# Four graph layers on one core: layer 1's output is computed by its width, and nodes 2p and 2p+1 share a partition

## The chip, the cores and the metric

The kernel runs on one core of a Trainium2 chip. The metric is device time in microseconds of one whole execution; the median of several executions is given. A profile is one execution with its instruction trace.

## The reference

64 graphs of 256 nodes with 512 features pass through four layers. Each layer normalises `x` by node, applies relu to give `h`, and adds the layer's result to `x`:

```python
h = jnp.maximum(_layernorm(x, axis=-1), 0.0)
x = x + layer(h, adj, ...)
```

Layers 0 and 3 compute one number per node from the adjacency matrix and two projections of `h`, take a softmax of it over the nodes, and scale a third projection, `v`, by it. Layer 2 has eight heads of 64 features: `tanh(A * (Xp C) Xp^T) Xp`, then relu.

Layer 1, which the change is mostly about, is attention with eight heads of 64 features:

```python
dense = leaky_relu(e_self[..., :, None] + e_neigh[..., None, :], 0.2) + NEG_BIG * (1.0 - A)
att = softmax(dense, axis=-1)
out = relu(einsum('bhij,bhju->bhiu', att, feats) + b)
```

`e_self` and `e_neigh` are one number per node and head. All data is float32.

## The kernel before

One graph is one pass of `graph(b)`, a set of named steps. Each step issues its instructions when it is called; the table `TIMES` gives each step a due time, and `Plan.run` calls the steps of all graphs sorted by `b * PERIOD + due`. On each engine and on SP's queue of transfers the instructions then run in just that order, so the table is the schedule: about five graphs are in flight, and only the order of the due times counts, not their values. Buffers (PSUM banks, tiles of x, and so on) come from fixed pools through `take` and go back with `done`, in that same order.

A graph's nodes lie on the partitions: chunk `c` of 128 nodes, node `128c + p` on partition `p`. Every layer begins with `normed`: `st`, `rs`, `sh` on VectorE (`bn_stats`, L314), `pw` on GpSimd (L325), `hn` on ScalarE (L337). TensorE needs `h` with the features on the partitions. That turn is made in three steps: `sq` turns 32 by 32 squares on VectorE (L270), `sw` writes them to device memory (L357, tile `sq_d`), and `ht` gathers them back in four transfers (L275). `rows` (L264) is the helper for all products of `ht` with a weight.

Layer 1's steps, in order:
- `fa`, `fb`, `fae`, `fbe`: the features and, in 16 more columns, `e_self` and `e_neigh`. `feats` carries a column of ones behind each head.
- `sendp`, `senda`, `er`, `enes`: TensorE turns the 16 columns into rows (L482), ScalarE copies them (L487), and SP writes them out and broadcasts them to all partitions.
- `max`, `mxv`, `mxp`, `mxa`, `mr`, `mb`: the row maximum on VectorE (L510), turned by TensorE (L531), copied (L536), written and broadcast.
- `ea` (ScalarE, L555), `eg` (GpSimd, L562), `eb` (VectorE, L568), `ex` (ScalarE, L574): the weights of two heads, with the source node on the partitions.
- `po` (TensorE, L586): the exponentials are the stationary operand, and 65 columns of `feats` (64 and the ones) move. The sum of a row thus falls out as the 65th column, with the output node on the partitions.
- `pn` (VectorE, L599 and L603) takes the reciprocal of the sums, and relu and product; `pa` (GpSimd, L611) adds to `x`.

Layer 2's `py` (L690) already works the other way round: features are stationary, 64 wide, two heads go to the two halves of the output's partitions, and 256 nodes move. Its output has the features on the partitions and is turned back by `sqy` (L724), `swy` and `yr` (L736), and added by `yg` and `yv` (L743). `xc` (L655) multiplies by layer 2's matrix C, with one 64 by 64 block for each head; `ps` (L676) are layer 2's scores.

Layers 0 and 3 end with `softp` (TensorE, L375), `softv`, `softa`, `softw` and `add` (L400), with the products `pv`; `z` and `zv` (L783) are layer 3's score. `load` and `store` are SP's transfers of `x` and the adjacency matrix. Before the first graph, ScalarE's queue loads the weights (L172 to L238), and TensorE multiplies the two halves of layer 3's weight.

Of the kernel before, what the change touches and what calls it, by code (L numbers as in the profile page):

```python
# [23 lines left out]
UE = U + 1  # L24
# [12 lines left out]
PERIOD = 60.200  # L37
TIMES = {
    "load": 0.000, "at": 1.247, "st0": 5.280, "rs0": 5.300, "negt": 7.670, "pw0": 13.367, "sh0": 13.387,
    "hn0": 13.407, "sq0": 13.427, "sw0": 16.594, "ht0": 18.551, "qk1": 23.168, "qk0": 24.945, "qe0": 24.965,  # L40
    "qe1": 24.985, "pv01": 25.815, "score0": 27.291, "s0v": 27.311, "softp0": 29.436, "pv00": 31.771,
    "softv0": 32.366, "softa0": 33.344, "softw0": 35.861, "add0": 35.881, "st1": 39.861, "rs1": 39.881,
    "pw1": 40.011, "sh1": 40.031, "hn1": 40.638, "sq1": 43.586, "sw1": 46.132, "ht1": 57.350, "fa0": 57.370,
    "fa1": 57.370, "fb0": 57.370, "fae0": 57.934, "fae1": 58.840, "sendp": 58.860, "senda": 58.880,
    "er": 60.959, "neg": 61.845, "fb1": 64.147, "fbe0": 67.381, "enes": 67.749, "fbe1": 71.535,
    "max2": 74.244, "ea1": 75.256, "max0": 75.757, "max3": 76.069, "ea3": 77.200, "ea0": 78.017,
    "max1": 78.219, "mxv": 78.317, "mxp": 79.925, "ea2": 80.651, "eg2": 82.397, "mxa": 85.102, "eg0": 86.489,
    "mr": 87.558, "eg1": 88.075, "mb": 88.185, "eb0": 90.739, "eb2": 93.202, "ex0": 94.320, "eb1": 95.449,
    "eg3": 96.405, "po0": 97.573, "ex1": 97.708, "ex2": 99.827, "po2": 100.283, "eb3": 101.293,
    "ex3": 101.313, "po1": 102.298, "pn0": 106.351, "pa0": 108.061, "po3": 110.560, "pn1": 110.580,  # L50
    "pa1": 114.029, "st2": 114.049, "rs2": 114.069, "pw2": 114.089, "sh2": 117.872, "hn2": 117.892,
    "sq2": 120.365, "sw2": 126.933, "ht2": 134.926, "xp0": 134.946, "xp1": 140.660, "xe0": 141.890,
    "xe1": 147.360, "sqx": 147.380, "swx": 148.833, "xpt": 152.315, "xc": 161.371, "xcv": 174.104,
    "ps0": 174.124, "xca": 174.124, "tv1": 174.144, "ta1": 174.164, "tv0": 174.656, "ta0": 177.182,
    "ps1": 177.255, "tv2": 177.275, "ta2": 178.752, "tv3": 180.071, "am": 180.091, "ta3": 180.091,
    "py0": 181.534, "py1": 184.516, "ye0": 188.391, "ye1": 188.411, "sqy": 190.648, "swy": 192.764,
    "yr": 197.444, "yv": 199.505, "yg": 201.580, "st3": 202.086, "rs3": 203.471, "pw3": 205.848,
    "sh3": 205.868, "hn3": 207.396, "sq3": 207.856, "agg0": 209.112, "sw3": 211.920, "ga0": 215.679,
    "agg1": 217.655, "ht3": 218.179, "ga1": 220.247, "z0": 234.444, "z1": 245.189, "zv0": 245.866,
    "pv30": 248.297, "pv31": 251.239, "zv1": 261.554, "softp3": 263.233, "softv3": 264.096,  # L60
    "softa3": 267.934, "softw3": 282.911, "add3": 285.241, "store": 294.897,
}


class Plan:

# [8 lines left out]
    def run(self, graph, count):  # L75
        graphs = {}
        for _, b, name in sorted((b * PERIOD + at, b, name) for b in range(count) for name, at in TIMES.items()):
            if b not in graphs:
                graphs[b] = graph(b)
            traced = self.tc.nc.cur_bb.bb.instructions  # L80
            n = len(traced)
            graphs[b].steps[name]()
            for i in traced[n:]:
                if i.engine in PINNED:
                    if i.engine in self.last:
                        self.tc.add_manual_dep(i, self.last[i.engine], mybir.DependencyInfo(
                            mybir.DependencyClass.NoSync, mybir.DependencyReason.DATA), reason="plan")
                    self.last[i.engine] = i.name
# [32 lines left out]
def tile_four_gnn_layers(ctx: ExitStack, tc: tile.TileContext, x, adj, nodemask,  # L121
# [4 lines left out]

    nc = tc.nc
# [7 lines left out]
    small = ctx.enter_context(tc.tile_pool(name="small", bufs=6))  # L135
# [4 lines left out]
    plan = Plan(tc)  # L140

# [11 lines left out]
    keep("blocks", 2, [P, NC, N // S, S])  # L153
    keep("feats", 2, [P, NC, H, UE])
# [5 lines left out]
    keep("o", 1, [P, NC, 4 * U])  # L160
    turn = [0]

    def passing(name):
        turn[0] += 1
        return plan.pools["bank"][4 + turn[0] % 4]

    def load_weight(name, src):
        t = consts.tile([P, KC, src.shape[1]], F32, name=name)  # L170
        for r in range(4):
            nc.scalar.dma_start(t[r::4], src.rearrange("(k r d) e -> r d k e", k=KC, r=4)[r])  # L172
        return t
# [5 lines left out]
    for f in plan.pools["feats"]:  # L179
        nc.gpsimd.memset(f[:, :, :, U:], 1.0)  # L180

    wqk0_s = load_weight("wqk0_s", wqk0)
    wv0_s = load_weight("wv0_s", wv0)
    w1a_s = consts.tile([P, KC, FA], F32)
    w1b_s = consts.tile([P, KC, D - HA * U], F32)
    for k in range(KC):
        for r in range(4):
            first = k * P + r * S
            w1_k = w1[:, first:first + S, :].rearrange("h d u -> d h u")
            nc.scalar.dma_start(w1a_s[r::4, k, E:].rearrange("p (h u) -> p h u", h=HA), w1_k[:, :HA])  # L190
            nc.scalar.dma_start(w1b_s[r::4, k].rearrange("p (h u) -> p h u", h=H - HA), w1_k[:, HA:])
    a_bc = once.tile([P, 2, D], F32, bufs=1)
    nc.scalar.dma_start(a_bc[:, 0, :], a_self.rearrange("h u -> (h u)").partition_broadcast(P))
    nc.scalar.dma_start(a_bc[:, 1, :], a_neigh.rearrange("h u -> (h u)").partition_broadcast(P))
    b1_bc = consts.tile([P, D], F32)
    nc.scalar.dma_start(b1_bc, b1.rearrange("h u -> (h u)").partition_broadcast(P))
    mask_rows = once.tile([B, N], F32, bufs=1)
    nc.scalar.dma_start(mask_rows, nodemask)
    w2_s = consts.tile([P, KC, H, U], F32)
    for k in range(KC):  # L200
        for r in range(4):
            first = k * P + r * S
            nc.scalar.dma_start(w2_s[r::4, k], w2[:, first:first + S, :].rearrange("h d u -> d h u"))
    b2_bc = consts.tile([P, D], F32)
    nc.scalar.dma_start(b2_bc, b2.rearrange("h u -> (h u)").partition_broadcast(P))

    c2_s = consts.tile([P, HP, U], F32)
    for s in range(2):
        nc.scalar.dma_start(c2_s[s * U:(s + 1) * U], c2t.rearrange("(a s) k j -> s k a j", s=2)[s])
    wv3_s = load_weight("wv3_s", wv3)  # L210

    for k in range(KC):
        for s in range(2):
            for first, w in ((0, w1a_s[:, k, E:]), (HA, w1b_s[:, k])):
                w = w.rearrange("p (h u) -> p h u", u=U)
                n = w.shape[1]
                prod = once.tile([P, n, U], F32, name="prod", bufs=1)
# [58 lines left out]
    def graph(b):  # L278
# [311 lines left out]
        for p in range(HP):  # L590
            attention(p)
# [237 lines left out]
```

## Time and profile before

| | |
|---|---|
| median of 3 executions | 3979.25 us (3978.55 to 3984.05) |
| profiled execution, its own time | 3981.05 us |
| its span in the trace | 3979.0 us |
| mean granted TensorE clock | 0.989 |
| busy: TensorE, VectorE, ScalarE, GpSimd | 96%, 76%, 43%, 32% |
| DMA packets | 1657995, of them 1494320 under 512 B; 717.69 MB |

The busy shares are of the whole span. A float32 matmul appears as two records in the trace, so counts of matmuls are twice those of the code; the turns by the identity appear once. A group line of the profile names the line, engine, operation and tiles, the shapes, the count, then busy time and mean duration, and last the engine's idle time before the group and what ended it. The timeline of SP lists transfers by the time at which SP issues them, and the second number there is what issuing took, not what the transfer took.

### The profile page before, as it was taken

The page shows a single profiled execution, that of the slowest core. Times are in us where ns is not written, and L with a number is a line of the kernel's source. Part 1 is how long each engine was busy: PE and PEld are TensorE (multiplying, and loading weights), DVE is VectorE, ACT ScalarE, POOL GpSimd, SP SyncE. Part 2 cuts the span into 40 slices and gives each one's busy share as a digit, 9 for nine tenths or more (in the row PEclk, how much of TensorE's full clock was granted, in tenths as well). Part 3 has the DMA queues.
Part 4 walks back from the last instruction along what each step waited for, and adds up shares of the span by engine and source line. Part 5 has one row for each costly group of instructions (what it writes and reads, how often), then busy time and mean ns, then how long its engine had stood idle before and what let it go on. Part 6 is the DMA issues. An engine that isn't in the chain of part 4 may idle for free.

```text
span 3979.0 us, 54683 instructions
## 1 busy us (share of the span) xinstructions
PE 3819.5 (96%) x17986; PEld 2345.2 (59%) x17986; DVE 3023.1 (76%) x7658; ACT 1708.5 (43%) x3333; POOL 1263.1 (32%) x1097
## 2 busy tenths in 40 slices
PE   3689999999999999999999999999999999999997
PEld 1456666656656656656656656656656656665653
DVE  2577878877877878777787787787787887887873
ACT  0344444444444444444444444444444444444442
POOL 0233333332332332332332332332333333333330
PEclk9799999999999999999999999999999999999999
DMA  4577777777877877777777777778777787787763
GB/s 112 136 181 177 195 194 180 192 189 188 185 186 191 187 186 188 185 190 190 178 192 185 181 192 189 176 193 193 171 196 193 175 195 191 180 193 188 184 159 79
DMA packets 1657995, 717.69 MB, mean 180 GB/s; under 512 B 1494320, under 2 KB 1549680, under 8 KB 1633136
## 3 DMA queue, kind: packets, MB, share of 16 engines
q1 hardware_dynamic: 1641472, 706.39, 72.8%
q10 hardware_dynamic: 16240, 7.80, 0.8%
q8 instruction: 144, 2.36, 0.3%
q14 instruction: 139, 1.14, 0.1%
HBM read 477.56 MB, written 236.45 MB: 179 GB/s over the span
## 4 chain that ended last, share of the span: by engine, by line
PE 83%; DVE 7%; DMA 4%; SPq 2%; issue 1%; POOL 1%; ACT 1%; ACTq 1%; POOLq 0%; DVEq 0%
PE bank L264 49%; PE bank L586 11%; PE bank L676 6%; PE bank L690 6%; PE bank L762 5%; PE bank L655 3%; DVE junk L510 3%; DVE sq L270 2%; DMA hn<-sq_d 1%; SPq L275 1%; PE bank L426 1%; DMA ht<-sq_d 1%; PE bank L375 1%; DVE shift L330 1%; POOL xt L743 1%
## 5 line engine op out<-in xcount | busy, mean ns | idle before, releaser
L264 PE MATMUL bank<-wv_s,ht 128*128 128x512 f32 x2048 | 910.8, 592 | 0.0
L264 PEld LDWEIGHTS bank<-wv_s,ht 128*128 128x128 f32 x2048 | 380.9, 191 | 428.6 <-issue 413.1
L562 POOL TENSOR_TENSOR pair<-pair,negt 128x1024 f32<-128x1024 f32 x256 | 598.7, 2361 | 28.7 <-ACT pair L555 28.7
L337 ACT ACTIVATE hn<-xt,shift,rstd 128x512 f32<-128x512 f32 x512 | 390.4, 809 | 458.2 <-DVE shift L330 443.1
L555 ACT ACTIVATE pair<-all,ec 128x256 f32<-128x256 f32 x1024 | 417.1, 496 | 222.1 <-DMA all<-er_d 222.1
L586 PEld LDWEIGHTS bank<-feats,pair 128*128 128x128 f32 x4096 | 473.0, 192 | 58.5 <-issue 53.9
L264 PE MATMUL bank<-w_s,ht 128*128 128x512 f32 x1024 | 466.1, 598 | 33.6 <-DMA ht<-sq_d 28.1
L715 ACT ACTIVATE pair<-pair 128x512 f32<-128x512 f32 x512 | 295.9, 625 | 452.1 <-DVE pair L708 452.1
L586 PE MATMUL bank<-feats,pair 128*128 128x65 f32 x4096 | 479.2, 275 | 2.7 <-ACT pair L574 2.7
L264 PE MATMUL bank<-m_s,ht 128*128 128x512 f32 x1024 | 468.5, 600 | 3.0 <-DMA ht<-sq_d 3.0
L510 DVE CUSTOM_DVE_ANT_0 junk<-all,adj 128x256 f32<-128x256 f32 x1024 | 432.4, 422 | 37.7 <-DMA all<-er_d 4.2
L325 POOL TENSOR_TENSOR rstd<-rstd,power 128x2 f32<-128x2 f32 x256 | 180.5, 705 | 829.1 <-DVE rstd L321 822.6
L708 DVE TENSOR_TENSOR pair<-bank,at 128x512 f32<-128x512 f32 x512 | 328.5, 684 | 127.4 <-PE bank L676 127.4
L743 POOL TENSOR_TENSOR xt<-xt,hn 128x512 f32<-128x512 f32 x64 | 111.7, 1746 | 957.1 <-DMA hn<-sq_d 711.2
L270 DVE STREAM_TRANSPOSE sq<-hn 128x512 f32<-128x512 f32 x512 | 338.1, 690 | 59.4 <-ACT hn L337 59.4
L314 DVE BATCH_NORM_STATS2 stats<-xt 128x6 f32<-128x512 f32 x512 | 327.6, 682 | 28.1 <-POOL xt L743 27.9
L264 PEld LDWEIGHTS bank<-w_s,ht 128*128 128x128 f32 x1024 | 189.2, 192 | 258.6 <-issue 209.8
L568 DVE TENSOR_TENSOR pair<-pair,all 128x1024 f32<-128x1024 f32 x256 | 328.0, 1301 | 0.0
L264 PEld LDWEIGHTS bank<-m_s,ht 128*128 128x128 f32 x1024 | 189.7, 190 | 213.7 <-issue 206.6
L611 POOL TENSOR_TENSOR xt<-xt,o 128x256 f32<-128x256 f32 x256 | 182.7, 725 | 331.2 <-DVE o L603 233.8
L264 PE MATMUL bank<-w1a_s,ht 128*128 128x272 f32 x1024 | 256.1, 404 | 23.6 <-DMA ht<-sq_d 23.6
L754 POOL TENSOR_SCALAR at<-at,mask_c 128x256 f32<-128x256 f32 x128 | 117.5, 927 | 497.7 <-DVE pair L708 497.7
(81 smaller groups left out, 4871.3 us busy)
## 6 DMA issues: line engine op xcount, KB each, us to landing
sq_d<-sq SPq DMA_DIRECT2D x384, 512.0 KB
ht<-sq_d SPq DMA_DIRECT2D x1024, 128.0 KB
all<-er_d SPq DMA_DIRECT2D x128, 1024.0 KB
all<-m_d SPq DMA_DIRECT2D x64, 1024.0 KB
xt<-in_x_dram SPq DMA_DIRECT2D x64, 512.0 KB
xpt<-sq_d SPq DMA_DIRECT2D x256, 128.0 KB
hn<-sq_d SPq DMA_DIRECT2D x256, 128.0 KB
out_dram<-xt SPq DMA_DIRECT2D x64, 512.0 KB
```

Source lines behind the costliest of these rows:

```text
L264: nc.tensor.matmul(p, ht[:, k, c * P:(c + 1) * P], w[:, k], start=(k == 0), stop=(k == KC - 1))
L270: nc.vector.transpose(sq.rearrange("p (r k c i) -> p c k r i", r=4, k=KC, c=NC)[:, c], t[:, c])
L314: nc.vector.bn_stats(stats[:, c, :], g["xt"][:, c, :])
L337: nc.scalar.activation(hn[:, c, :], g["xt"][:, c, :], AF.Relu, bias=st["shift"][:, c:c + 1], scale=st["rstd"][:, c:c + 1])
L510: nc.vector.tensor_tensor_reduce(junk, g["en"][:, h, :], g["adj"][:, c, :], 1.0, -BIG, OP.add, OP.max, st["mx"][:, c, h:h + 1])
L555: nc.scalar.activation(e[:, s, j, :], g["es"][:, h, :], AF.Prelu, bias=st["ec"][:, j, H + h:H + h + 1], alpha=0.2)
L562: nc.gpsimd.tensor_tensor(e, e, g["negt"][:, None].to_broadcast([P, 2, NC, N]), OP.add)
L568: nc.vector.tensor_tensor(e, e, g["m"][:, 2 * p:2 * p + 2, None, :].to_broadcast([P, 2, NC, N]), OP.subtract)
L586: nc.tensor.matmul(po[:, h % 4, :], e[:, s, j, i * P:(i + 1) * P], feats[:, j, h, :], start=(j == 0), stop=(j == NC - 1))
L676: nc.tensor.matmul(ps[s][:, m, :], g["xpt"][half, p, m * P:(m + 1) * P], g["xc"][half, p, :], start=True, stop=True)
L708: nc.vector.tensor_tensor(th[:, s], g[f"ps{p}{s}"].rearrange("p (m n) -> p m n", m=NC), g["at"], OP.mult)
L715: nc.scalar.activation(g[f"th{p}"][:, s], g[f"th{p}"][:, s], AF.Tanh)
```

## The change

- Node `2p + c` lies on partition `p` as chunk `c`. So two neighbouring nodes share a partition, the rows of `x` and of the adjacency matrix are read and written as one run for each partition, and the gathers move runs of 64 elements for 32. A chunk of nodes within a free dimension is now every second element (`chunk`). The 32 by 32 turns write or read in steps of two elements.
- `po` has the features stationary, 64 columns on one half of the output's partitions, and moves the 256 exponentials, like `py`. The column of ones goes. The row sums come from a new matmul, `su`, with a column of ones in a stationary operand of 32 columns; GpSimd first adds the two halves of the source nodes (`eh`). Each pair of a head's position and r has its own 32 output partitions.
- ScalarE takes the output out of PSUM with relu (`oe`), and `back`, now shared with layer 2, turns it to the nodes: `sqo` (VectorE), `swo` and `or` (SP). The sums are copied (`se`), turned by TensorE (`sp`), and inverted by VectorE (`sr`). GpSimd multiplies and adds to `x` (`oa`).
- The score rows and the maxima are turned by VectorE's 32 by 32 transposes (`send`, `mxt`) in place of TensorE and a copy by ScalarE; `er` and `mr` then write in four transfers for one.
- `xc` uses one 128 by 128 block with two heads on its diagonal for two 64 by 64 blocks.
- The weights' steps are issued from SP's queue ahead of the first graph, in a table `WEIGHTS`; before, they were issued from ScalarE's queue.
- Two scratch tiles go (the softmax exponentials and the score products are written over their PSUM source), `small` pools have 5 buffers for 6, and all due times are new, with `PERIOD` 59.0 for 60.2.

```diff
-PERIOD = 60.200
+PERIOD = 59.0
 TIMES = {
...
+    "fa0": 67.715, "fa1": 67.725, "fae0": 67.735, "fae1": 70.445, "send": 70.465, "er": 70.485, "enes": 70.505,
...
+    "ex0": 105.783, "eb2": 106.779, "ex3": 108.073, "po0": 109.204, "eg1": 110.015, "ex2": 111.923, "eb1": 113.549,
+    "po2": 113.901, "eh0": 114.929, "ex1": 117.816, "po1": 117.836, "eh1": 117.837, "oe0": 117.856, "su0": 118.502,
+    "eh3": 118.704, "po3": 119.010, "eh2": 119.242, "su1": 119.262, "oe1": 120.178, "sqo": 120.198, "se": 122.147,
+    "swo": 124.057, "sp": 125.389, "sr": 125.409, "or": 127.489, "oa1": 132.474, "oa0": 135.453, "st2": 135.705,
+    "rs2": 135.725, "pw2": 135.745, "sh2": 135.765, "hn2": 135.785, "sq2": 137.857, "sw2": 137.877, "ht2": 144.252,
...
+    "agg1": 237.211, "ga1": 241.253, "zv0": 241.622, "z1": 250.036, "zv1": 254.364, "softp3": 254.784,
...
+    "store": 284.217,
 }
...
+    def chunk(t, c):
+        return t.rearrange("p (n c) -> p c n", c=NC)[:, c]
...
+    def rows(p, ht, c, w):
+        for k in range(KC):
+            nc.tensor.matmul(p, chunk(ht[:, k], c), w[:, k], start=(k == 0), stop=(k == KC - 1))
+    def squares(sq, t):
+        for c in range(NC):
+            nc.vector.transpose(sq.rearrange("p (r k i c) -> p c k r i", r=4, k=KC, c=NC)[:, c], t[:, c])
+    def gathered(t, sq_d):
+        for i in range(4):
+            nc.sync.dma_start(t.rearrange("p k (b e) -> b p k e", b=4)[i],
+                              sq_d.rearrange("(b d) (r k e) -> b (d r) k e", b=4, r=4, k=KC)[i])
...
+        def back(name, cols):
+            @step(f"sq{name}")
+            def _():
+                nc.vector.transpose(g.take("sq").rearrange("p (b k c i) -> p k b c i", b=4, k=HP, c=NC),
+                                    g[cols].rearrange("p k (b i c) -> p k b c i", b=4, c=NC))
...
+            @step(f"{name}r")
+            def _():
+                y = g.take("hn", NC, name="y" if name == "y" else "yo")
+                y = y.rearrange("p c d -> p (c d)").rearrange("p (a f) -> p a f", a=4)
+                for q in range(4):
+                    nc.sync.dma_start(y[q * S:(q + 1) * S], st["sq_d"].rearrange("(a i) (q f) -> q i a f", a=4, q=4)[q])
...
+        @step("send")
+        def _():
+            st["er"] = er = work.tile([P, N // 4], F32, name="er", bufs=1)
+            nc.vector.transpose(er.rearrange("p (i c) -> p c i", c=NC), st["ec"])
...
-                    po = g[f"po{q}{i}"][:, :4 * UE].rearrange("p (q u) -> p q u", q=4)
                     for s in range(2):
                         h = 2 * p + s
-                        for j in range(NC):
-                            nc.tensor.matmul(po[:, h % 4, :], e[:, s, j, i * P:(i + 1) * P], feats[:, j, h, :],
-                                             start=(j == 0), stop=(j == NC - 1))
+                        nc.tensor.matmul(po[s * U:(s + 1) * U, p % 2, :], feats[:, j, h * U:(h + 1) * U],
+                                         e[:, s, j, :], start=(j == 0), stop=(j == NC - 1))
...
+            @step(f"eh{p}")
+            def _():
+                e = g[f"e{p}"]
+                nc.gpsimd.tensor_tensor(g.take("half", name=f"h{p}"), e[:, :, 0, :], e[:, :, 1, :], OP.add)
...
+            @step(f"su{q}")
+            def _():
+                if not q:
+                    g.take("bank", name="su")
+                for r in range(2):
+                    for s in range(2):
+                        t = 2 * r + s
+                        nc.tensor.matmul(g["su"][t * S:(t + 1) * S, :N], ones[:, q], g[f"h{2 * q + r}"][:, s, :],
+                                         start=(q == 0), stop=(q == 1))
...
+            @step(f"oe{q}")
+            def _():
...
+                nc.scalar.activation(g["oc"][:, 2 * q:2 * q + 2, :], g[f"po{q}"].rearrange("p (r n) -> p r n", r=2),
+                                     AF.Relu)
...
+        def divide(c):
+            @step(f"oa{c}")
+            def _():
+                y = g["yo"].rearrange("p c d -> p (c d)").rearrange("p (a k c i) -> p c k a i", a=4, k=HP, c=NC)[:, c]
+                rs = st["rs"][:, c].rearrange("p q t -> p (q t)").rearrange("p (k s) -> p s k", s=2)
+                for s in range(2):
+                    half = y[:, :, 2 * s:2 * s + 2]
+                    nc.gpsimd.tensor_tensor(half, half, rs[:, s, :, None, None].to_broadcast([P, HP, 2, S]), OP.mult)
+                xt = g["xt"][:, c, :].rearrange("p (k a i) -> p k a i", k=HP, a=4)
+                nc.gpsimd.tensor_tensor(xt, xt, y, OP.add)
```

## The prediction

> **What bounds the kernel now.** I read the page's engine shares first, then the table of windows, the chain of waits through one period, the timeline of SP, and the groups by line.
>
> ```profile
> PE 3819.5 (96%) x17986; PEld 2345.2 (59%) x17986; DVE 3023.1 (76%) x7658; ACT 1708.5 (43%) x3333; POOL 1263.1 (32%) x1097
> ```
>
> ```profile
> 1000.00:2000.00 1000.00, 994.83 (x4743) 613.73 (x4742) 792.17 (x1993) 447.30 (x872) 335.30 (x289) 1.00 0.77 187
> ```
>
> TensorE is busy 99.5% of the middle of the run at clock 1.00. VectorE follows with 79%, DMA with 77%. Busy matmuls are pipelined, so I take what a step adds to the chain:
>
> ```profile
> 2028.45 3.52 PE bank L586 x32
> 2031.97 1.87 PE bank L655 x16
> 2033.84 3.72 PE bank L586 x32
> 2037.56 1.93 PE bank L676 x16
> 2039.49 3.63 PE bank L264 x8
> ...
> 2050.63 0.22 PE bank L482 x2
> 2050.85 3.60 PE bank L690 x32
> ```
>
> A float32 matmul is two records, so `x32` is 16 matmuls. Adding all steps of one graph in this way (pv 4 x 3.44, xp 2 x 3.44, z 2 x 3.44, fa 2 x 1.83, fb 2 x 1.72, qk 2 x 0.89, score0 0.84, agg 2 x 1.75, the softmax turns 0.44, po 7.24, xc 1.87, ps 2 x 1.93, py 3.60, sendp and mxp 0.44) gives **58.2 us of TensorE work per graph**. The x loads of graphs 5 and 63 are issued at 323.6 and 3761.4 in SP's timeline: 58 periods, **59.27 us each**. 541 us lie outside them (fill 324, drain 217). So only 1.1 us per period is not TensorE work. A second limit is close:
>
> ```profile
> 2094.21 0.33 SPq L357 DMA_DIRECT2D sq_d<-sq  x1
> 2096.93 3.80 SPq L275 DMA_DIRECT2D ht<-sq_d  x4
> 2100.83 0.66 SPq L286 DMA_DIRECT2D xt<-in_x_dram  x1
> ```
>
> ```profile
> PE bank L264 <- DMA ht<-sq_d: 56.7, 16, 15.4
> ```
>
> The tile of squares sent out at 2094.21 can be gathered 2.72 us later, the gather takes 3.80 us to issue, and fa0 starts at 2104.99 (TensorE's timeline), just after it lands. The last line (list of waits) is TensorE waiting for such gathers: 57 us in all. The order written by hand leaves little slack behind softp0.
>
> ```profile
> L270 DVE STREAM_TRANSPOSE sq<-hn 128x512 f32<-128x512 f32 x512 | 338.1, 690 | 59.4 <-ACT hn L337 59.4
> L270 DVE STREAM_TRANSPOSE sq<-xp 128x512 f32<-128x512 f32 x128 | 136.6, 1107 | 0.0
> L611 POOL TENSOR_TENSOR xt<-xt,o 128x256 f32<-128x256 f32 x256 | 182.7, 725 | 331.2 <-DVE o L603 233.8
> L743 POOL TENSOR_TENSOR xt<-xt,hn 128x512 f32<-128x512 f32 x64 | 111.7, 1746 | 957.1 <-DMA hn<-sq_d 711.2
> ```
>
> These are prices for the new steps: a transpose read in runs and one read in steps of 4 elements, and GpSimd's adds.
>
> **What the Trainium skill says.** "TensorE: Matmul & The Clock Gate", Part 3, has matmuls that write distinct 32-column groups run concurrently, and in its section on LDWEIGHTS a load costs its columns over 1.2 GHz, 107 ns for 128. The trace agrees: L586 moves 65 columns but starts every 110 to 116 ns, about one load; L690, on two column halves, every 112 ns where an unsplit 256-column matmul takes 215 (1.72 us for 8). Four groups are not shown here. "SBUF — State Buffer", Door 1, says that float32 keeps full rate while two accesses fall in a 16-byte line. The 16-byte step of `xp` costs 1107 against 690 ns, which fits; an 8-byte step is not shown. "DMA: Bandwidth & Descriptors", "Why small descriptors are slow", gives each packet a fixed overhead; 1,494,320 of 1,657,995 packets here are under 512 B.
>
> **The change, part by part, per graph.**
>
> *TensorE.* po: 32 matmuls of 65 columns (7.24 us) become 16 of 256 columns on halves, the form of L690: 3.60. Gone are sendp and mxp, 0.44. sp is two transposes, 0.22. su is 8 matmuls (16 records) with 32 output columns: four at a time 16 x 54 = 0.9 us, as halves 1.8, one after the other 16 x 215 = 3.4; I take 0.9. xc, 16 records of 117 ns, becomes 8 of 215: 1.72 against 1.87. Sum: -7.24 - 0.44 + 3.60 + 0.22 + 0.9 - 0.15 = **-3.1 us, to 55.1** (57.6 with the dearest su). Stationary operands are now read in steps of 8 bytes (ht, at, xpt). Lower bound nothing; upper bound a doubled load, which would show where loads set the pace: 16 records of qk, 8 of score0, 32 of ps, each +107 ns, +6.0 us. I take nothing, by the SBUF page.
>
> *VectorE.* Out: four reciprocals of 179 and four L603 of 425 ns, -2.4. In: sqo 1.25 (L724's mean), send and mxt some 0.2 each, sr two at 0.18: +2.0. It stays at 47 us, which fits in any period above 55. The strided writes of the squares are taken as free; at worst they cost the 0.42 us of the step-of-4 read on each of eight transposes, twice that on sqo and sqy and 0.4 on at: +5.4, and VectorE would set about 57 to 58.
>
> *ScalarE.* Two oe at 0.60 and se 0.45, less 0.72 for the two row copies: +0.9 on 27, under TensorE. If that cover were gone, oe1 alone lies in the way back, 0.6.
>
> *GpSimd.* Four eh of 128x512 at half of L562's 2361: +4.7 (5.8 at L611's pace). oa: four 128x256 products at 0.73 and two adds at 1.75: +6.4; pa goes, -2.9. From 19.7 to 28 us, half busy. eh1 stands before su0, but TensorE then waits for ht1 anyway; oa is on a path (below).
>
> *Queues.* SP issues 42 transfers per graph before and 53 after: swo 1, or 4, er and mr 3 more each. At 0.35 to 0.7 us that is about 6 us more on a queue that issues for some 27. The load now stands before sw1 and ht1, so its 1 MB goes ahead of them, and swo, or and sw0 stand between ht1 and er. The five gathers and the adjacency blocks move 256 B runs for 128 B: 22,500 of the 25,900 packets per graph halve, the way back adds 1 MB in about 650 larger ones, so some 15,300 remain. DMA's 45 us per graph falls, I estimate to 35 to 40; at worst it keeps its length plus 1 MB at 187 GB/s spread, 5 us.
>
> *The new loop.* In the new order VectorE has sq1, tv1, st0, tv0, sqo; later st2, rs2, sh2, zv1; and softp3 waits for zv1. One period's path, at the durations of before: softp0 to the end of sq1 9.3 (9.9 in VectorE's timeline, 2084.3 to 2094.2, less part of an eb); then sw1, ht1's issue and tv/st0/sqo side by side 5.4; swo to or 2.7; or's issue and landing 5.9 (2.2 and 3.7 for y in the trace); oa 6.4; st2, rs2, pw2, sh2 2.9; zv1 0.9; softp3 0.25; TensorE from pv31 over pv30, fb1, xp, qk, pv00, score0, pv01 to the next softp0 25.2. **Sum 59.0 us.** Of it the gathers' issue and landings shrink with the halved packets: ht1 about 0.7, or 0.7, tot. 1.4, so **57.6**. What is late next is ht1 before fa0: between them TensorE has only 17.5 us of work after softp0, and softp0, sq1, sw1, ht1 take 9.3 + 2.7 + 5 to 6.5 = 17 to 18.5.
>
> *Start.* The weights move from ACT's queue to SP's, ahead of graph 0's load: some 50 issues of 0.65 us, so its x lands near 55. Before, hn0 waited until 53.6 behind the same issues on ScalarE, and qk0 ran at 73.8. I count -5 to +10 there and -10 for a shorter fill and drain (store due at 284 against 295): 530 us outside the 58 periods.
>
> **Sum.** 530 + 58 x 57.6 = 3871 us. The profiled execution took 3981.05, 2.05 over its span and 1.8 above the median of 3979.25; both cancel. I predict **3870 us**.
>
> **Rivals.**
> 1. The loop is slack because DMA lands sooner than I count, and TensorE stays the bound: 55.1 plus today's 1.1 = 56.2, so 530 + 58 x 56.2 = **3790**. For it: 99.5% busy now, DMA lighter. Against: the ht wait above, already there.
> 2. Slower: layer 1's way back (swo, or, oa) grows. Its point is a period over 59.4, which is 1.8 us above my sum. y landings of 5.0 to 5.2 us stand in the chain view beside my 3.7, and GpSimd's products could run at L743's pace with its strided halves, 4 x 0.15 more, while eh holds up pw. With +3 us, 60.6: **4045**. For it: every leg is on the path and in order. Against: 0.6 to 1.3 us of packet relief not counted elsewhere.
> 3. The regrouping doesn't run in parallel or its strided loads are dear: su serial gives 57.6 + 1.1 = 58.7, **3935**; doubled loads 61 and more, over 4070. The SBUF page speaks against the second.
>
> **How the numbers follow.** Loop-bound near 57.6, 3820 to 3930: 0.46. Rival 1, 3770 to 3820: 0.22. Rival 3 with slow su or strided VectorE: 0.10, nearly all under 3970. Rival 2 with doubled loads: 0.22, of which 0.05 falls within 0.2% of today and the rest beyond. About 8 us, 0.2%, is what a measurement of this kernel can tell from no change. So faster 0.77, same 0.05, slower 0.18; the range 3775 to 4000 leaves out the long tails, with 3820 to 3930 as the likeliest case's own.
>
> **What would show it.** Right: TensorE some 55 us of work per graph with small waits at fa0 for ht and at softp3 for VectorE; loads every 57 to 58 us; about 1.0 million packets; GpSimd about 45% busy. su records spaced near 54 ns confirm the grouping, 190-ns weight loads the strides, 690-ns squares the writes. It is wrong if loads come over 59.3 us apart, if VectorE's L603 is replaced by slower transposes, or if TensorE shows stalls over 5 us a period.

## The result, and the profile after

The changed kernel takes **4281.13 us** (median of 4 executions, 4274.33 to 4284.9), the kernel before 3981.65 beside it: ratio 1.0751, 95% interval 1.0732 to 1.0769. It is slower by 7.5% where 3870 us was predicted. The profiled execution's span is 4283.1 us.

The page of the kernel after, and further down its window; a window's columns are sum, then busy time of TensorE, its weight loads, VectorE, ScalarE and GpSimd, then clock, DMA share and GB/s:

```profile
PE 3815.1 (89%) x16322; PEld 2112.1 (49%) x16322; DVE 3239.5 (76%) x7449; ACT 1750.2 (41%) x3397; POOL 1775.1 (41%) x1484
...
DMA packets 967434, 784.72 MB, mean 183 GB/s; under 512 B 788912, under 2 KB 859120, under 8 KB 942576
...
DVE 32%; PE 24%; DMA 18%; POOL 9%; issue 7%; SPq 7%; ACT 3%; DVEq 0%; POOLq 0%; ACTq 0%
```

The last line has the shares of the chain of work that ended last. In the kernel before they were:

```profile
PE 83%; DVE 7%; DMA 4%; SPq 2%; issue 1%; POOL 1%; ACT 1%; ACTq 1%; POOLq 0%; DVEq 0%
```

The window after:

```profile
1000.00:2000.00 1000.00, 922.13 (x3945) 509.94 (x3943) 786.16 (x1822) 423.99 (x826) 432.42 (x355) 0.98 0.61 190
```

Of the packets 42% are gone (1657995 before), and DMA's share fell from 0.77 to 0.61, which is 39 us a graph for 46, so the transfers did get lighter. TensorE went from 99.5% busy to 92%, and VectorE, at 32% for 7%, is now the largest part of the chain. The x loads of graphs 5 and 63 are issued at 331.3 and 4035.0: 58 periods of **63.86 us** against 59.27, which is 266 of the 300 us. The rest lies outside: 579 us against 541, 30 of the 38 behind the last load.

Two of the waits of TensorE (total us, times, longest us); the second was 5.0 us in 12 times before:

```profile
PE bank L342 <- DMA ht<-sq_d: 141.4, 89, 20.9
PE bank L454 <- DVE bank L532: 131.5, 62, 9.5
```

L454 is `softp0`, L532 is `s0v`: once in each graph TensorE waits some 2 us for VectorE. What VectorE does ahead of `s0v`, in its timeline of one period, and GpSimd at that time:

```profile
2034.81 2.10 DVE L852 TENSOR_TENSOR xt<-xt,hn 128x512 f32<-128x512 f32 x1
...
2042.53 1.90 DVE L409 SCALAR_TENSOR_TENSOR shift<-mv,rstd 128x2 f32<-128x2 f32 x1
2044.36 4.50 DVE L651 TENSOR_TENSOR pair<-pair,all 128x1024 f32<-128x1024 f32 x2
2048.78 0.22 DVE L532 SCALAR_TENSOR_TENSOR bank<-bank,qk 128x64 f32<-128x64 f32 x1
...
2049.31 1.30 DVE L348 STREAM_TRANSPOSE sq<-hn 128x512 f32<-128x512 f32 x2
```

```profile
2034.01 5.12 POOL L645 TENSOR_TENSOR pair<-pair,negt 128x1024 f32<-128x1024 f32 x2
...
2042.06 5.71 POOL L645 TENSOR_TENSOR pair<-pair,negt 128x1024 f32<-128x1024 f32 x2
```

`yv` (L852) lasts 2.10 us where its mean before was 0.69; the `shift` of two elements 1.90, with a mean of 0.68 before; two `eb` (L651) 4.50, where two of the means before make 2.60. Each of them runs beside a pair of GpSimd's mask adds `eg` (L645). Three operations are thus 4.5 us longer in one stretch than at the means of before, and `s0v`, `softp0` and `sq3` (the last line) stand behind it. The page's groups, whose lines in the kernel before had 690 ns for the squares:

```profile
L645 POOL TENSOR_TENSOR pair<-pair,negt 128x1024 f32<-128x1024 f32 x256 | 690.9, 2720 | 31.5 <-ACT pair L638 31.5
...
L651 DVE TENSOR_TENSOR pair<-pair,all 128x1024 f32<-128x1024 f32 x256 | 439.4, 1736 | 11.3 <-DMA all<-m_d 11.3
...
L348 DVE STREAM_TRANSPOSE sq<-hn 128x512 f32<-128x512 f32 x512 | 341.2, 696 | 18.9 <-ACT hn L416 18.7
...
L669 PE MATMUL bank<-pair,feats 128*64 128x256 f32 x2048 | 289.9, 406 | 7.4 <-ACT pair L657 7.4
```

In the middle of the run before, `eb` took 1301 ns and `eg` 2359. The squares with their new strided writes hardly grew. One period later the chain that ended last (start, length) goes through the same operations:

```profile
2098.70 2.18 DVE xt L852
...
2106.48 1.26 DVE shift L409
2107.74 0.59 issue
2108.33 4.50 DVE pair L651 x2
...
2113.43 1.16 DVE sq L348 x2
2114.61 3.83 DMA sq_d<-sq
...
2123.20 3.68 PE bank L342 x8
```

From `sq3` it goes on through device memory to `z0`, the last line.

### The profile page after: what moved, and what is told of

It reads as the page before. It is cut to its first block, busy times and chain, and to the rows that moved or that the text cites. A ratio compares the mean times of both kernels' runs of the same rounds, so it can differ in the third digit from the quotient of the medians.

```text
span 4283.1 us, 53024 instructions
## 1 busy us (share of the span) xinstructions
PE 3815.1 (89%) x16322; PEld 2112.1 (49%) x16322; DVE 3239.5 (76%) x7449; ACT 1750.2 (41%) x3397; POOL 1775.1 (41%) x1484
## 4 chain that ended last, share of the span: by engine, by line
DVE 32%; PE 24%; DMA 18%; POOL 9%; issue 7%; SPq 7%; ACT 3%; DVEq 0%; POOLq 0%; ACTq 0%
PE bank L342 11%; DMA sq_d<-sq 7%; DVE pair L651 6%; PE bank L669 5%; DVE junk L599 5%; DMA ht<-sq_d 5%; DVE sq L348 4%; DMA hn<-sq_d 4%; POOL xt L737 4%; DVE stats L393 4%; POOL hn L735 3%; SPq L353 3%; DVE xt L852 3%; PE bank L871 3%; SPq L499 2%
## 5 line engine op out<-in xcount | busy, mean ns | idle before, releaser
L342 PE MATMUL bank<-w_s,ht 128*128 128x256 f32 (+2 forms) x3072 | 940.2, 460 | 76.6 <-DMA ht<-sq_d 61.0
L342 PEld LDWEIGHTS bank<-w_s,ht 128*128 128x128 f32 x3072 | 598.2, 198 | 390.1 <-issue 303.5
L645 POOL TENSOR_TENSOR pair<-pair,negt 128x1024 f32<-128x1024 f32 x256 | 690.9, 2720 | 31.5 <-ACT pair L638 31.5
L678 POOL TENSOR_TENSOR half<-pair 128x512 f32<-128x512 f32 x256 | 323.6, 1274 | 410.5 <-PE bank L692 242.3
L651 DVE TENSOR_TENSOR pair<-pair,all 128x1024 f32<-128x1024 f32 x256 | 439.4, 1736 | 11.3 <-DMA all<-m_d 11.3
L852 POOL TENSOR_TENSOR xt<-xt,hn 128x512 f32<-128x512 f32 x64 | 81.5, 1274 | 692.5 <-DMA hn<-sq_d 577.7
L657 ACT ACTIVATE pair<-pair 128x1024 f32<-128x1024 f32 x256 | 261.8, 1047 | 201.2 <-DVE pair L651 201.2
L735 POOL TENSOR_TENSOR hn<-hn,rs 128x256 f32<-128x256 f32 x256 | 152.1, 615 | 456.6 <-DMA hn<-sq_d 309.4
L871 PE MATMUL bank<-hn,at 128*128 128x512 f32 x512 | 288.0, 691 | 21.0 <-ACT hn L416 21.0
L669 PE MATMUL bank<-pair,feats 128*64 128x256 f32 x2048 | 289.9, 406 | 7.4 <-ACT pair L657 7.4
```

Source lines behind the costliest of these rows:

```text
L342: nc.tensor.matmul(p, chunk(ht[:, k], c), w[:, k], start=(k == 0), stop=(k == KC - 1))
L645: nc.gpsimd.tensor_tensor(e, e, g["negt"][:, None].to_broadcast([P, 2, NC, N]), OP.add)
L651: nc.vector.tensor_tensor(e, e, g["m"][:, 2 * p:2 * p + 2, None, :].to_broadcast([P, 2, NC, N]), OP.subtract)
L669: nc.tensor.matmul(po[s * U:(s + 1) * U, p % 2, :], feats[:, j, h * U:(h + 1) * U], e[:, s, j, :], start=(j == 0), stop=(j == NC - 1))
L678: nc.gpsimd.tensor_tensor(g.take("half", name=f"h{p}"), e[:, :, 0, :], e[:, :, 1, :], OP.add)
L871: nc.tensor.matmul(pg, chunk(g["at"][:, m], c), g["hn"][:, m, :], start=(m == 0), stop=(m == NC - 1))
```

## The experiments

Theory W: the new way back of layer 1 (`swo`, `or`, `oa`) makes the period long. Theory O: the new order does, by putting two turns through device memory into one loop. Theory T, formed after the first eight runs: the new order puts VectorE's operations on two SBUF tiles beside GpSimd's, and these take turns. "Period" is always worked out as above. The expectations, written before each run, name their theories by letters of their own. The `before` of a comparison ran on the same chip.

### The parts of the change apart

`layout_old_times` has the node layout, the turned score rows, `xc`, the weights' queue, but the old output and the old due times:

```diff
-            new output: po by width, eh, su, oe, se, sp, sr, back("o", "oc"), oa
+            old output: po with 65 columns moving, pn, pa
-PERIOD = 59.0     (and TIMES of the changed kernel)
+PERIOD = 60.200   (and TIMES of before; send 58.86 for sendp/senda, mxt 79.925 for mxp/mxa)
```

> Everything of the change but layer 1's output by its width and the new due times: po, pn and pa as before, due times and period as before (send and mxt in the places of sendp and mxp). Theory A (the period is set by one loop through layer 1's new way back, swo, or, oa, and the queues it blocks): no way back, so 3930 to 3985 us, the lower end if the halved packets help. Rival D (the new layout, strided reads or the weights on SP's queue cost the time): over 4100. Rival B (GpSimd's added work slows VectorE) and rival C (the new due times are bad in themselves): about 3980.

Measured: **3945.63 us, ratio 0.9891 (0.9877 to 0.9906)**, period 58.71. The windows:

```profile
1000.00:2000.00 1000.00, 999.59 (x4570) 643.38 (x4569) 803.61 (x2067) 444.78 (x850) 339.67 (x293) 1.00 0.63 189
```

TensorE is almost never idle and DMA has fallen to 0.63. This part of the change is a gain of 1.1%; it ends below both kernels.

`old_out_new_times` keeps the new due times and takes the output back:

```diff
+TIMES.update({"pn0": 117.9, "pa0": 117.95, "po2": 118.0, "pn1": 120.178, "pa1": 120.19})
-            new output
+            old output (no eh, su, swo, or, oa)
```

> The changed kernel with layer 1's output the old way (po, pn, pa as before, pn and pa at the due times of oe, po2 moved behind po1 so that the banks suffice), at the new due times. A: without the way back 3900 to 4050 us. B: the same, since eh and oa are gone. C (the new due times are bad in themselves): 4150 to 4300.

Measured: **4373.89 us, 1.0965 (1.0947 to 1.0983)**, period 65.16. With no way back at all it is slower still, so the loss doesn't need the way back: theory W falls. Its groups have the same long operations:

```profile
L668 POOL TENSOR_TENSOR pair<-pair,negt 128x1024 f32<-128x1024 f32 x256 | 688.3, 2710 | 36.5 <-ACT pair L661 36.5
...
L674 DVE TENSOR_TENSOR pair<-pair,all 128x1024 f32<-128x1024 f32 x256 | 438.8, 1734 | 6.9 <-DMA all<-m_d 6.9
```

`half_mask_add` leaves the mask out for one of the two heads of each pair:

```diff
-                nc.gpsimd.tensor_tensor(e, e, g["negt"][:, None].to_broadcast([P, 2, NC, N]), OP.add)
+                nc.gpsimd.tensor_tensor(e[:, 0], e[:, 0], g["negt"], OP.add)
```

> The changed kernel with GpSimd's mask addition eg done for one of each pair's two heads: some 5 us less GpSimd work per graph, and that where VectorE's yv and eb run slow. A: the slowed yv and eb are legs of the loop, so 1 to 3 us per graph, 4090 to 4220 us. B (contention is the main cause): 4 to 5 us per graph, 3960 to 4030. C: no change, 4270 to 4290.

Measured: **4101.31 us, 1.0281 (1.0265 to 1.0298)**, 180 us less than the changed kernel. `eb`'s mean falls to 1474 ns and TensorE's wait for L532 from 131.5 to 4.9 us. The length of the mask adds on GpSimd, 41% busy, thus lies in the loop.

`late_st2` puts `st2` to `sw2` behind `zv1`, `ye`, `softv3`, `sqy`, `softw3` and `swy`:

> The changed kernel with other due times only: st2, rs2, pw2, sh2, hn2, sq2 and sw2, which wait for layer 1's way back, come behind zv1, ye, softv3, sqy, softw3 and swy on their engines, still ahead of max. A: TensorE's softp3 and layer 2's way back no longer wait for oa, so 2 to 4 us per graph less, 4030 to 4160 us. B: no change, 4260 to 4290. C says only that some order is better.

Measured: **4698.25 us, 1.1778 (1.176 to 1.1795)**, the opposite of what theory O wanted: TensorE's wait for `ht` rises to 534.1 us. The way from `st2` over `sw2` and `ht2` to `xp0` has no slack, so delaying it costs; taking its place behind `zv1` frees nothing.

### Is it the turn through memory that bounds?

```diff
+TIMES.update({"z0": 237.2})     # z0 behind po3: late_z0, and late_z0_half_mask with the edit above
```

> The changed kernel with one due time altered: z0, layer 3's score product (four matrix multiplies), comes on TensorE right behind po3 of the next graph instead of ahead of its po1. All work is kept. Theory A (one loop holds both turns through device memory): in the changed kernel z0 waits 1.74 us for ht3, and po1, po3, oe1 and with them layer 1's way back, sq2 and ht2 stand behind it, while ht3 itself stands behind sq3, which stands behind what xp0 and ht2 let go. With z0 behind po3 the leg through ht3 is out of the loop, so the loop is shorter by z0's wait (1.7 us) and its own run (1.2 us), less what is late next: 1.5 to 2.9 us a graph, 4281 falls to 4110 to 4195 us. Theory B (by-width work itself is slow, in contention of VectorE and GpSimd, wherever z0 stands): within 30 us of 4281.

> late_z0 with the mask added by GpSimd to one of the two heads of each pair alone (the other head's part is left out), which took 180 us from the changed kernel. If the mask add and the slower VectorE beside it lie in the same loop as z0's wait, and that loop still bounds late_z0, the two gains add up: 4281 - 180 - (90 to 170) = 3930 to 4010 us, unless TensorE's own 55 to 56 us a graph (some 3800 us in all) comes first. If taking z0 out leaves another loop as the bound in which no mask add lies, it stays near late_z0.

Measured: **4276.5 us, 1.0732 (1.0716 to 1.0748)** and **4113.82 us, 1.0325 (1.0301 to 1.0349)**. `z0`'s wait of 1.74 us can be taken away and nothing is won, and the half mask brings what it brought without it. The waits of `late_z0`:

```profile
PE bank L456 <- DVE bank L534: 135.5, 63, 10.0
PE bank L671 <- ACT pair L659: 121.4, 66, 4.5
```

The first is `softp0` for `s0v`, nearly unchanged. The second has grown from 7.4: `po` now waits for `ex`, which stands behind `eb` and `eg`. Theory O in this form falls.

`other_due_times` has all of the changed kernel's work with due times in which `z`, `zv`, `xc`, `ps` and `tv` come some 10 us later against `po`:

> All of the changed kernel's work, with other due times and a period of 58.74: layer 3's z0, z1, zv0, zv1 and layer 2's xc, ps, tv stand some 10 us later against po0 to po3 and layer 1's way back, and z0 comes on TensorE behind po3, so that neither turn through device memory has a product of the next graph's layer 1 waiting behind it. Theory A (the order, not the by-width work, made the change slow): TensorE nearly fills the period again, at 56 to 58.5 us a graph: 530 to 590 us outside and 58 periods give 3780 to 3980 us, likeliest 3900. Theory B (by-width output costs more than it saves in any order, through GpSimd's added 8 us and the slower VectorE beside it): over 4100 us.

Measured: **4297.64 us, 1.0788 (1.0771 to 1.0806)**: not faster, though almost every step moved. Its page:

```profile
L726 DVE CUSTOM_DVE_ANT_0 junk<-all,adj 128x256 f32<-128x256 f32 x1024 | 764.6, 747 | 44.9 <-DMA all<-er_d 13.7
...
L778 DVE TENSOR_TENSOR pair<-pair,all 128x1024 f32<-128x1024 f32 x256 | 300.5, 1217 | 10.9 <-DMA all<-m_d 10.9
```

`eb` is at 1217 ns now, and `max` (L726), 434 ns in the changed kernel, is at 747: 16 x 0.31 = 5 us a graph. The loss seems to have moved to another operation on two SBUF tiles; that this sets the time here was not tried by itself. This run gave theory T.

`no_products` leaves the four products of `oa` out:

```diff
-                    nc.gpsimd.tensor_tensor(half, half, rs[:, s, :, None, None].to_broadcast([P, HP, 2, S]), OP.mult)
```

> The changed kernel without the four products by the reciprocal sums in oa0 and oa1 on GpSimd (the division is left out; the two adds to xt stay). oa is a leg of the way back (5.0 us in one period of the trace, some 2.4 us of it products). If the loop through layer 1's way back sets the period, it falls by 2 to 2.6 us a graph: 4281 - 58 x 2.3 = 4150 us (4120 to 4175). If the loop doesn't pass through oa, within 30 us of 4281.

Measured: **4239.57 us, 1.0639 (1.0623 to 1.0654)**, 42 us less and a third of what was expected. The way back is a small part of the loop.

### The turns by themselves

`beside` runs six forms of VectorE's operations, alone and beside mask adds of GpSimd.

> The disputed cost by itself: none of the layers is computed (all tiles are zeros). VectorE runs each of six forms of its operations 12 times with GpSimd idle, GpSimd runs its 1024-column mask add 12 times with VectorE idle, and then each of the six forms runs 24 times beside 16 mask adds. The forms are: the 1024-column subtract of two SBUF tiles (eb), the 512-column product of a PSUM and an SBUF tile (tv), the 256-column add with a maximum over two SBUF tiles (max), the 512-column transpose of one SBUF tile (sq), the two-element product of two SBUF tiles (shift), and the statistics of one SBUF tile (st). Theory A (VectorE operations that read two SBUF tiles and GpSimd's operations take turns, so that where they meet their times add): eb, max and shift last longer beside GpSimd (eb from 1.3 us to 2.2 or more, max from 0.43 to 0.7 or more), and the mask adds beside them go from 2.36 us to 2.7 or more; tv, sq and st keep their times within 5%. Theory B (all traffic to SBUF slows by a common share): all six grow alike, by 10 to 40%. Theory C (no contention: the longer means in the changed kernel come from something else, such as waits counted into the operation): all six within 5%.

The timeline of VectorE, first alone, then beside 16 mask adds each (second column: length of the stretch):

```profile
7.89 15.07 DVE L148 TENSOR_TENSOR pair<-pair,m 128x1024 f32<-128x1024 f32 x12
...
31.46 0.42 DVE L156 CUSTOM_DVE_ANT_0 junk<-en,adj 128x256 f32<-128x256 f32 x1
...
36.94 8.92 DVE L160 STREAM_TRANSPOSE sq<-hn 128x512 f32<-128x512 f32 x12
45.78 2.27 DVE L164 SCALAR_TENSOR_TENSOR shift<-mv,rstd 128x2 f32<-128x2 f32 x12
...
86.87 62.50 DVE L148 TENSOR_TENSOR pair<-pair,m 128x1024 f32<-128x1024 f32 x24
...
193.19 2.44 DVE L156 CUSTOM_DVE_ANT_0 junk<-en,adj 128x256 f32<-128x256 f32 x1
...
233.31 17.88 DVE L160 STREAM_TRANSPOSE sq<-hn 128x512 f32<-128x512 f32 x24
...
273.06 27.05 DVE L164 SCALAR_TENSOR_TENSOR shift<-mv,rstd 128x2 f32<-128x2 f32 x24
```

and of GpSimd, alone and beside the 24 `eb`:

```profile
57.35 28.93 POOL L144 TENSOR_TENSOR gp<-gp,negt 128x1024 f32<-128x1024 f32 x12
...
88.22 52.51 POOL L144 TENSOR_TENSOR gp<-gp,negt 128x1024 f32<-128x1024 f32 x16
```

Where the two run beside each other (count: shortest, median, longest in ns):

```profile
L148 DVE TENSOR_TENSOR pair<-pair,m x15: 3244/3245/3246, 89.4 to 135.3; 128x1024 f32<-128x1024 f32 x15
L144 POOL TENSOR_TENSOR gp<-gp,negt x15: 3198/3201/3202, 91.6 to 137.5; 128x1024 f32<-128x1024 f32 x15
```

Alone an `eb` takes 1.26 us (15.07 / 12) and a mask add 2.41 (28.93 / 12). Side by side they go one for one, a pair in 3.28 us (52.51 / 16). Free of each other a pair would take 2.41, one after the other 3.67. So their times add up but for 0.4 us: most of the time, while one engine works, the other stands. A `max` of 0.42 us lasts 2.44, a whole mask add; a `shift` has a mean of 1.13 in place of 0.19. The transposes (0.74 each), the product from PSUM (0.72) and the statistics (0.73) keep their times. Theory T holds for the forms, the common slowdown of theory B does not.

### Taking the turns out, and putting them in

`apart_times` again has all of the changed kernel's work; only due times and the period (59.187) differ, though nearly all of them. Some, with the shift against the changed kernel:

```diff
+    "eg0": 97.61 (0), "eg3": 106.03 (+8.5), "eb0": 106.82 (+4.2), "eg2": 109.10 (+6.1), "eb2": 112.42 (+5.6),
+    "eb3": 112.66 (+10.6), "ea1": 116.27 (+22.8), "eg1": 117.87 (+7.9), "eb1": 120.42 (+6.9), "eh2": 138.16 (+18.9),
+    "max0": 90.03 (+3.7), "yg": 212.2 (+1.6), "yv": 221.3 (+7.6), "z0": 240.24 (+4.4)
```

> All of the changed kernel's work, with due times and a period (59.19) chosen so that eb, max and yv on VectorE do not meet eg, eh, oa and yg on GpSimd: eg0, eg2 and eg1 come right behind or well before eb, eh2 and eh3 behind ht1, and max behind the mask adds; z0 stays behind po3. Theory A (the new due times, not the by-width work, cost the time, because they put VectorE's operations on two SBUF tiles beside GpSimd's, where the two take turns: 1.75 us for eb where it takes 1.26 alone, 2.17 for yv against 0.70): eb's mean falls to 1.2 to 1.35 us, max stays at 0.42, yv under 1.3, and with the by-width output's 1.5 to 3 us less on TensorE it ends below the kernel with the old times and old output (3946): 3840 to 3950 us, likeliest 3890. Theory B (the by-width output itself costs the time): eb falls as said, and the time stays over 4100 us.

Measured: **4009.27 us, 1.0059 (1.0042 to 1.0076)**, period 59.37. The windows, and the group of `eb`:

```profile
1000.00:2000.00 1000.00, 975.62 (x4264) 550.34 (x4261) 793.27 (x1954) 461.32 (x894) 455.45 (x383) 1.00 0.65 204
```

```profile
L778 DVE TENSOR_TENSOR pair<-pair,all 128x1024 f32<-128x1024 f32 x256 | 305.8, 1215 | 13.6 <-DMA all<-m_d 10.0
```

`eb` is at 1215 ns, `yv` at 692, `max` at 422 in the middle of the run; 272 of the 300 us have come back with the same instructions. As other steps moved too, this run alone doesn't give all 272 to the turns. And 4009 lies above the 3840 to 3950 that theory A had, and 64 us above the old output in `layout_old_times`: even in the best order tried here the by-width output is slower than the old output at the old times.

> apart_times with the mask added by GpSimd to one of the two heads of each pair alone (the other head's part is left out). The same edit took 180 us from the changed kernel. Theory A (what counted there was taking turns, not GpSimd's own time): where the two engines are kept apart the edit brings less than 40 us. If the mask add is a leg of the loop as such: 100 to 200 us again.

Measured: **3968.23 us, 0.9954 (0.9939 to 0.9969)**. Half of the mask add was worth 180 us in the changed kernel and is worth 41 where the engines are kept apart, just over the 40 that theory A had set. What counted was mostly the turns, not GpSimd's own time.

`layout_idle_adds` does the reverse and puts turns into the good order:

```diff
+                for _ in range(2):
+                    nc.gpsimd.tensor_tensor(scrap, scrap, scrap, OP.add)     # ahead of each of the four max steps
```

> The kernel with the old output and old due times (3945.6 us) and one addition: ahead of each of the four max steps GpSimd adds a 512-column SBUF tile to itself twice, eight adds a graph of some 1.27 us, 10.2 us on an engine that is busy 34% of the time. Nobody reads the tile and nobody waits for it. Theory A (turns): the adds meet VectorE's max, which waits out about one add each as in the measurement by itself (2.44 us where it takes 0.42), so up to eight of the sixteen max of a graph last some 1.2 us longer, VectorE's way from er to mr grows by 5 to 10 us, and the time rises by 2 to 6 us a graph: 4060 to 4300 us. Theory C (no turns, or slack takes them up): 3940 to 3980 us.

Measured: **4169.66 us, 1.0459 (1.0443 to 1.0476)**. Work on an engine that was 34% busy, for which nobody waits, costs 224 us against `layout_old_times`:

```profile
L614 DVE CUSTOM_DVE_ANT_0 junk<-all,adj 128x256 f32<-128x256 f32 x1024 | 764.7, 747 | 39.3 <-DMA all<-er_d 5.9
```

`max` goes from 423 to 747 ns.

### Which meeting the period runs through, and TensorE's price

```diff
+TIMES.update({"eb3": 103.583})     # late_eb3: 102.083 before; eb3 comes behind s0v
```

> The changed kernel with one due time altered by 1.5: eb3, one subtract of a pair on VectorE, comes behind s0v instead of ahead of eb0 and s0v. All work is kept. In the changed kernel eb3 and eb0 run as one stretch of 4.50 us beside GpSimd's mask adds where they take 2.5 alone, and s0v, for which TensorE's softp0 waits (131.5 us in all), sq3, sw3 and ht3 stand behind both. Theory A (the loop runs through these turns on VectorE): softp0 and sq3 come about one contended eb earlier, 2 to 3 us a graph, and 4281 falls to 4095 to 4170 us. Rival (the two gathers behind sw2 and sw3 set the period, wherever eb3 stands): within 40 us of 4281.

Measured: **4098.02 us, 1.0273 (1.0251 to 1.0295)**, period 60.77. One due time, moved by 1.5, brings 183 us. VectorE's timeline of one period:

```profile
2021.15 1.91 DVE L411 SCALAR_TENSOR_TENSOR shift<-mv,rstd 128x2 f32<-128x2 f32 x1
2022.99 1.21 DVE L653 TENSOR_TENSOR pair<-pair,all 128x1024 f32<-128x1024 f32 x1
2024.12 0.22 DVE L534 SCALAR_TENSOR_TENSOR bank<-bank,qk 128x64 f32<-128x64 f32 x1
...
2024.65 1.30 DVE L350 STREAM_TRANSPOSE sq<-hn 128x512 f32<-128x512 f32 x2
2025.87 1.65 DVE L653 TENSOR_TENSOR pair<-pair,all 128x1024 f32<-128x1024 f32 x1
```

`eb0` fits between two mask adds, `s0v` follows at once, and by the time of `eb3` the mask adds are nearly done: `eb`'s mean is 1327 ns. The `shift` still takes its 1.9 us.

`outputs_alone` measures TensorE alone; four stretches of eight rounds, and nothing waits:

> TensorE's price of the two outputs by itself: none of the layers is computed (tiles of zeros, nothing waits). Four stretches of eight rounds. The first has 16 of the 512-column products a round; the second the same and the old output (64 products of 65 columns a round); the third the same 16 and the new output (32 products of 256 columns on half of the columns); the fourth 28 of the 512-column products, the new output, the sums (8 products on 32 columns) and the two transposes of the sums. Prediction's step (3.64 us a graph saved on the output, 0.9 paid for the sums and 0.22 for their turn): second less first 7.2 us a round, third less first 3.6, fourth less third and less 12 products 1.1. Rival (switching between tilings of TensorE adds to each group, so that the new output with its sums saves a microsecond or less): third less first 4.5 or more, the sums and their turn 1.8 or more.

```profile
12.48:123.37 110.89, 110.43 (x251) 48.88 (x252) 0.41 (x2) 0.00 (x0) 1.00 0.00 0
123.37:293.32 169.95, 169.95 (x769) 108.95 (x768) 0.42 (x1) 0.00 (x0) 1.00 0.00 1
293.32:441.96 148.64, 148.64 (x513) 61.50 (x512) 0.42 (x1) 0.00 (x0) 1.00 0.00 0
441.96:689.68 247.72, 247.68 (x854) 101.80 (x852) 0.43 (x2) 0.00 (x0) 1.00 0.00 0
```

(The expectation counts the outputs in records, two to a product.) A round: 16 products alone 13.86 us, or 0.87 each; the old output (169.95 - 110.89) / 8 = **7.38 us**; the new output (148.64 - 110.89) / 8 = **4.72**; the sums and their turn (247.72 - 148.64) / 8 - 12 x 0.87 = **1.99**. The new output with its sums costs 6.71 and saves 0.67 us a graph. The rival of this run holds in its amount; whether switching between tilings is the reason was not tried.

## Why the prediction was wrong, point by point

**The step that failed first** is the loop sum, which was made "at the durations of before", with VectorE that "stays at 47 us": it had 57.6 us, and the period took 63.86. The durations were taken from an order in which `eb` and `eg` hardly meet. In the new order they do. The loop's last leg, `softp3` to the next `softp0`, was put at 25.2 us and took 29.1 in the period above. In it TensorE waited 1.70 us for `ht2`, ahead of `xp0`, and 1.83 for `s0v`; `yv`, `shift` and `eb`, which lie on VectorE ahead of `s0v`, are 1.4 + 1.2 + 1.9 us longer there than at the means of before. That VectorE's stretch ahead of `s0v` lay on the loop at all the sum did not have: it followed TensorE there. `late_eb3` shows that it does (-183 us), `half_mask_add` that GpSimd's mask add is behind it (-180), `beside` what the operations do to each other, and with the meetings taken out, among other moves, `apart_times` has 272 us less. VectorE's mean for a graph was 0.786 x 63.86 = 50.2 us.

A second leg grew as much. From `softp0` to the end of `sqo` the sum had 9.3 + 5.4 = 14.7 us, by way of `sq1`; in the next period it took 19.2, from the first to the last of these lines:

```profile
2049.11 0.72 PE L454 MATMUL bank<-ident,wc 128*128 128x128 f32 x2 [1.83 <-DVE bank L532]
...
2059.18 3.68 PE L342 MATMUL bank<-m_s,ht 128*128 128x512 f32 x8 [1.74 <-DMA ht<-sq_d]
...
2067.02 1.25 DVE L486 STREAM_TRANSPOSE sq<-cols 128x1024 f32<-128x1024 f32 x1 [1.75 <-ACT cols L701]
```

`sqo` waited for `oe1`, which stood behind `po3` and `z0` on TensorE, and `z0` for `ht3`, whose squares `sq3` stand behind `eb` and `s0v` on VectorE. The sum had no way through `sq3` and `z0`. Taking `z0` out of it brought nothing (`late_z0`), where `po` then waited for `ex`, which stands behind `eb` and `eg`.

The rule was to be had: the Trainium skill, "SBUF — State Buffer", section "Who interferes with whom", says that a VectorE instruction with two SBUF inputs contends with a GpSimd instruction that reads SBUF, and that whoever is first holds the pair of ports for the whole instruction. `beside` agrees in which of the six forms grow, with 2.44 us for a `max` of 0.42; but with `eb` and the mask add 0.4 of 3.67 us did overlap. The prediction read another section of the same page for its strides and did not use this one.

**TensorE at 55.1 us was wrong too.** By the windows it was busy 0.9948 x 59.27 = 58.96 us a graph before, 58.69 in `layout_old_times`, and 0.9756 x 59.37 = 57.9 in `apart_times`. The output was predicted at 3.60 and the sums and their turn at 1.12; `outputs_alone` has 4.72 and 1.99. The saving on the output, the sums and their turn together was 7.24 - (3.60 + 0.9 + 0.22) = 2.5 us in the prediction; it is 0.67. So rival 1 (3790 us) could not have come either: it needed 55.1.

**Rival 2** (a way back that grows) is not what happened: in that next period `swo` to `or` and `or` to `oa` took 2.8 and 4.5 us (2.7 and 5.9 counted) and `oa` 5.0 (6.4 counted), and the kernel without a way back is slower. The slower side, 0.18 of the chances, came by a mechanism that was not among the rivals. **Rival 3** is refuted in its second half: weight loads went from about 191 to between 197 and 201 ns with the strides, and the eight records of one group of `su` take 0.57 us, 71 ns each, where 215 was counted for one after the other, so the groups do run beside each other, if not at 54.

**What was right:** the packets (0.967 million for 1.0), GpSimd's share (43% in mid-run for 45), the strided writes of the squares (696 ns), the start (`qk0` at 69.9 us for 73.8). The layout, the score rows on VectorE, `xc` and the weights' queue together are a gain of 1.1%, as `layout_old_times` shows; it saves 0.3 us of TensorE by the windows, and takes away nearly all of its idle time. What each of them gives was not tried.

**What stays open:** the 38 us more outside the 58 periods, where the prediction had 11 less. `layout_old_times` has 541 us there, `apart_times` 563, so about 22 go with the new output or its due times; which, no run tells. The granted clock: in the middle of the run it was 0.98, where the kernel before and `apart_times` have 1.00. An estimate from these figures: TensorE lost some 0.02 x 63.9 = 1.3 us of full clock in a period, and up to that much of the 4.6 us more may be slower products. Whether the lower clock is a part of the loss or only comes with TensorE's waits, no run tells.

## What to carry to other kernels

A duration from a profile belongs to its order: before an operation on two SBUF tiles is moved, look at what GpSimd does at that time, and add the two, nearly in full, where they meet (3.28 us for 1.26 and 2.41 in `beside`). An engine at 41% can be a leg of the loop, and work for which nobody waits is not free (224 us in `layout_idle_adds`). When a new order is slow, list the operations whose means have grown (`eb` 1.30 to 1.75, `yv` 0.69 to 2.17) before following waits: the waits pointed at device memory and at TensorE, and moving `z0` out of their way did nothing.

## What the runs showed of the hardware that was not expected

- The `shift` of two elements pays too: it follows `pw` on GpSimd, whose next instruction is often a mask add, so that it lasts 1.9 us where each of twelve in a row took 0.19 alone. In the kernel before its mean was already 683 ns.
- GpSimd mask adds that meet one short `max` after another lose little (39.71 us for 16 against 38.6), while each `max` loses 2 us. Beside `eb` both lose: 0.87 us for each mask add, 2 us for each `eb`.
- Small groups of products on a part of TensorE's columns, between products on all of them, cost more than as many in one row: 32 records in four groups add 4.72 us in `outputs_alone`, where the 32 of `py` took 3.60 in the kernel before.
